# A two-layer attention and convolution kernel: position rows loaded by head, the second image issued from GpSimd, and the last 64 transform rows computed in quarters

## The chip, the core and the metric

The kernel runs on one core of one Trainium2 chip. The metric is the device time in microseconds (us) of one execution. A core has five engines with queues of their own, and in the trace an engine's instructions follow the order of its queue: TensorE (PE, matmuls; its weight loads are listed as PEld), VectorE (DVE), ScalarE (ACT), GpSimd (POOL) and SyncE (SP, which here only issues DMAs). ACT and POOL can issue DMAs too. SPq, ACTq and POOLq are an engine's sequencer, which issues DMAs and waits for semaphores.

## The reference

Two images of 128 channels and 64x64 pixels go through two layers. All data are fp32.

```python
# layer 0, on group-normalised x
y = _ln(x, g1, be1)                    # per pixel, over channels
y = _na2d(y, ...)                      # attention of each pixel to its 7x7 neighbourhood, 4 heads of 32,
                                       # with a position bias rpb[head, row offset, column offset]
y = _ln(y, g2, be2) @ w1.T + bl1; x = y + r
y = relu(_ln(x, g3, be3) @ w2.T + bl2); y = _ln(y, g4, be4) @ w3.T + bl3; x = y + r
# layer 1, on tokens t (2 x 4096 x 128)
t = t + softmax(q q^T / sqrt(128), diagonal masked) q      # q = _ln_t(t), over an image's 4096 tokens
t = t + sum over 4 branches of weight * stu(_ln_t(t)[:T/frac])   # long causal convolution with 16 filters,
                                       # by a Fourier transform, then two 128x128 matrices per filter
```

The position bias of layer 0 has 13x13 values for each head.

## The kernel before

**Layer 0** goes through 16 bands: two images, eight bands of eight image rows each. A band has 512 pixels, cut in eight tiles of 8x8; two tiles make a unit (u0 to u3). The work on a band is written as small pieces, functions with names such as `p.tok` (transpose to tokens, L327 inside `to_tokens`), `p.bn` and `p.pw` (statistics on DVE and POOL, L378 to L386), `p.za`, `p.zd` (normalise on ACT, L406, and on DVE, L415), `p.tr`, `p.zT` (transpose back, L189, and copy, L428), `p.v`, `p.q`, `p.k` (products, L466 and L332), `p.vc`, `p.qT`, `p.kT` (their copies, L474, L451, L460), and for each unit `S` (scores for four heads, L506), `t` and `e` (add the table and take the minimum on DVE, L519; exponential on ACT, L529), `T` and `c` (transpose, L542, and copy, L549) and `V` (values, L564). The order is written out by hand: PLAN gives each piece a place within a period of 2300 units for each band, and FIRST a place ahead of all for those of the first bands and for the preparations. The events are sorted by place, and PE, DVE, ACT and POOL execute them in this order. SP's DMAs follow as their data and buffers allow.

`p.vc` stores a band's v to DRAM in eight DMAs (L476), and `windows` loads for each unit the 14x14 key windows of its two tiles from there in four DMAs (L493, `vw`, six buffers). A window needs rows of the bands on both sides.

The bias is used as a table `tab` (128 queries x 196 keys) for each of six positions of a unit and each head: mask minus a shifted piece of `base`. `base` is made once per head by `flipped` (L248, the pieces `f0` to `f3`): PE multiplies `rev`, 64 shifted copies of the padded bias rows, by a flip matrix (L249), and ACT copies the result (L253). `rev` has one partition for each of the 64 query offsets, and for each head and row 20 values. It is loaded by 16 DMAs of short rows of 80 bytes (L291, L293), after two memsets. `table` (L258) makes the tables: the pieces `tab0` to `tab3` on DVE, `tab` (12 tables in 16 operations) on POOL. `weights`, `weights_kept` and `behind` fold the gains and offsets of the norms into the weights: products with one column (L721, L725) and, in `behind`, L760, L761 and L769 with small copies on DVE (L753 to L770).

The first image is loaded by four DMAs on SP at the very start (L127); group_norm takes statistics of it (L340). The second image is loaded by `second`, four DMAs on ACT's queue (L796), at place 1000.

**Layer 1** computes attention for one image after the other in pairs of 512-token chunks (L898 scores, L905 exponential, L912 transposes, L926 and L951 sums), all matmuls on PE. Between these steps `fill` puts other work: the rest of layer 0, the filters, `filter_matrices` (loads `st` on SP, mixed on DVE, L1107 to L1121), and `after`, which finishes the four tiles of 128 tokens of a chunk: divide and add (L980), normalise, transpose, and the forward transform. This transform has 320 rows, in two halves (q) of 64 input tokens: for 256 of them there are four matmuls 64x128 by 512 columns (L1011), copied on DVE for q = 0 and on ACT for q = 1 (L1013), and stored (L1000). The last 64 rows are these lines; `pu` is one PSUM bank, and `after` runs 16 times in all:

```python
pu = bank()
for q in range(2):
    rows_ = slice(q * SB, (q + 1) * SB)
    nc.tensor.matmul(pu[rows_], lhsT=tr[rows_, h, 2 * P : NC], rhs=z2[rows_], start=True, stop=True)   # L1019
ub = sp.tile([P, 512], F32, tag="ub", name="ub", bufs=3)
nc.scalar.copy(ub, pu)                                                                                  # L1021
for q in range(2):
    store(2 * P, q, ub[q * SB : (q + 1) * SB])
```

The convolution in the frequency domain follows (L1306 products with the filters, L1307 copies, L1318 the filter matrices), then the inverse transform and the output.

Of the kernel before, what the change touches and what calls it, by code (L numbers as in the profile page):

```python
# [8 lines left out]
F32 = mybir.dt.float32  # L9
# [5 lines left out]
P = 128  # L15
# [5 lines left out]
HEADS, DH, KW = 4, 32, 7  # L21
# [9 lines left out]
W_QKV, W_PROJ, W_1, W_2, W_3 = 0, 384, 512, 640, 768  # L31
V_G1, V_BE1, V_G2, V_BE2, V_G3, V_BE3, V_G4, V_BE4, V_QB, V_KB, V_BL3 = range(11)
R_VB, R_PROJ, R_BL1, R_BL2 = range(4)
RPW = 128


QT, WN, NTAB = 8, 14, 20
# [2 lines left out]
BAND = QT * GW  # L40


RPR = NTAB + 1

# [23 lines left out]


FIRST = (
    "gn p.xg0 p.xg1 p.tok0 p.tok1 w p.bn0 p.bn1 p.pw0 p.pw1 p.zd0 p.nb0 p.za0 p.tr0 p.zd1 p.nb1 p.za1 wd p.xg2 p.zT0 f0"
    " p.tr1 f1 p.v0 p.q0 p.k0 p.zT1 p.vc0 p.qT0 tab0 p.kT0 f2 f3 tab p.v1 p.k1 p.q1 tab1 p.vc1 p.kT1 p.qT1 tab2 tab3"
).split()
PHW = P + TH

# [4 lines left out]
SB = CB // SG  # L82
NC = CB + SB
# [10 lines left out]
def kernel(  # L94
# [16 lines left out]
    nc = tc.nc  # L111
# [18 lines left out]
    tt, tok, cm = [None, None], [None, None], [None, None]  # L130
# [4 lines left out]
    space = tok[0].rearrange("p n c -> p (n c)")  # L135
    base = space[:, 0 : HEADS * NTAB * NTAB].rearrange("p (h n m) -> p h n m", h=HEADS, n=NTAB)
    mask = space[:, HEADS * NTAB * NTAB : HEADS * NTAB * NTAB + 6 * KEYS].rearrange("p (c k) -> p c k", k=KEYS)
    rev = cm[0][0 : QT * QT, 0 : HEADS * RPR * NTAB].rearrange("p (h n m) -> p h n m", h=HEADS, n=RPR)

    ident = const.tile([P, P], F32, name="ident")  # L140
    make_identity(nc, ident)
# [4 lines left out]
        out=flip, in_=flip, compare_op=ALU.not_equal, fill=1.0, base=1 - QT * QT, pattern=[[0, 2], [1, QT * QT]],  # L146
# [73 lines left out]
    with l0a:  # L220
# [26 lines left out]
        def flipped(h):  # L247
            pb = l0_bank()  # L248
            nc.tensor.matmul(  # L249
                pb[:, 0 : NTAB * NTAB], lhsT=flip.rearrange("p a q -> p (a q)"),  # L250
                rhs=rev[:, h, 0:NTAB].rearrange("p n m -> p (n m)"), start=True, stop=True,
            )
            nc.scalar.copy(base[:, h].rearrange("p n m -> p (n m)"), pb[:, 0 : NTAB * NTAB])  # L253

        def table(ci, h, eng):
            n0 = (6, 0, 3)[ci // 2]
            for hp, m0 in ((slice(0, 64), 6), (slice(64, P), 0)) if ci % 2 == 0 else ((slice(0, P), 3),):
                eng.tensor_tensor(  # L258
                    tab[hp, ci, h].rearrange("p (n m) -> p n m", m=WN),
                    mask[hp, ci].rearrange("p (n m) -> p n m", m=WN),  # L260
                    base[hp, h, n0 : n0 + WN, m0 : m0 + WN], ALU.subtract,
                )
# [15 lines left out]
        )  # L278
        gavg = gavg.rearrange("p g r -> p (g r)")


        nc.gpsimd.memset(rev[:, 0].rearrange("p n m -> p (n m)"), 0.0)
        nc.gpsimd.memset(rev[:, HEADS - 1, NTAB], 0.0)
        nc.sync.dma_start(out=mask, in_=nc.inline_tensor(_window_masks(), "window_masks").ap())
        for r in range(QT):
            lo = 6 - min(r, 6)
            src = bass.AP(
                rpb_pad.tensor, (RPR + r - 6) * RPW + 50, [[1, QT], [RPW, (HEADS - 1) * RPR - r // 7], [1, NTAB]]
            )
            rows_ = rev[r * QT : (r + 1) * QT].rearrange("p h n m -> p (h n) m")  # L290
            (nc.scalar if r % 3 == 2 else nc.sync).dma_start(out=rows_[:, RPR : HEADS * RPR - r // 7], in_=src)  # L291
            src = bass.AP(rpb_pad.tensor, (lo + r - 6) * RPW + 50, [[1, QT], [RPW, RPR - lo], [1, NTAB]])
            nc.scalar.dma_start(out=rows_[:, lo:RPR], in_=src)  # L293
        wg = w_sb
        cb = wp.tile([P, 5], F32, name="cb")
        C_Q, C_K, C_V, C_1, C_3 = range(5)
# [476 lines left out]
        events = []  # L773
        for k, (b, g) in enumerate(order):
            t = {}
            for name, at in PLAN.items():
                if name[0] == "k" and b == 0:
                    continue

                at = FIRST.index(f"{name}{k}") - 1000 if f"{name}{k}" in FIRST else at + k * PERIOD  # L780
                events.append((at, k, name, lambda f=pieces[name], t=t, b=b, g=g: f(t, b, g)))
        for name, f in (
            ("gn", lambda: [None for _ in group_norm(0)]), ("w", weights), ("wd", weights_kept),
            *((f"f{h}", lambda h=h: flipped(h)) for h in range(HEADS)),
            *((f"tab{h}", lambda h=h: table(0, h, nc.vector)) for h in range(HEADS)),
            ("tab", lambda: [table(ci, h, nc.gpsimd) for ci in (1, 4, 5) for h in range(HEADS)]),
        ):
            events.append((FIRST.index(name) - 1000, None, "", f))
        for i in range(8):
            events.append((2 * PERIOD + 600 * i, None, "", lambda ci=2 + i // 4, h=i % 4: table(ci, h, nc.gpsimd)))  # L790
        rest_ = behind()
        for i in range(4):
            events.append((150 + 350 * i, None, "", lambda: next(rest_)))
        def second():
            for c in range(4):
                nc.scalar.dma_start(out=xa[1][:, c * 1024 : (c + 1) * 1024], in_=xin[1, :, c * 1024 : (c + 1) * 1024])  # L796

        events.append((1000, None, "", second))

        gn1 = group_norm(1)  # L800
        for i in range(7):
# [55 lines left out]
    with ap_:  # L857
# [6 lines left out]
        def bank():  # L864
            return ps_m.tile([P, 512], F32, tag="bank", name="bank")
# [102 lines left out]
        def after(b, c, part):  # L968

            n0 = 4 * c  # L970
            ph, f0 = divmod(n0, FB)
            par, h = divmod(ph, 2)
            pt = bank()
            for j in range(4):
                nc.tensor.transpose(pt[:, j * P : (j + 1) * P], xa[b][:, (n0 + j) * P : (n0 + j + 1) * P], ident)
            rden = sp.tile([P, 4], F32, tag="rden", name="rden")
            nc.vector.tensor_reduce(rden, part[:, n0 : n0 + 4, :], AX.X, ALU.add)
            nc.vector.reciprocal(rden, rden)
            for j in range(4):
# [15 lines left out]
            yield  # L995
            z2 = z.rearrange("p f d -> p (f d)")

            def store(m0, q, src):
                mn = min(P, NC - m0)
                nc.sync.dma_start(  # L1000
                    out=us[m0 // 2 : (m0 + mn) // 2, :, 2 * h + q, f0 : f0 + 4, b, par, :].rearrange(
                        "g r f d -> (g r) f d"
                    ),
                    in_=src.rearrange("p (f d) -> p f d", d=P),
                )

            for m0 in (0, P):
# [3 lines that stand above are left out]
                    nc.tensor.matmul(pu, lhsT=tr[rows_, h, m0 : m0 + P], rhs=z2[rows_], start=True, stop=True)  # L1011
                    ub = sp.tile([P, 512], F32, tag="ub", name="ub", bufs=3)
                    (nc.scalar.copy if q else nc.vector.tensor_copy)(ub, pu)  # L1013
                    store(m0, q, ub)
                yield
            pu = bank()
            for q in range(2):
                rows_ = slice(q * SB, (q + 1) * SB)
                nc.tensor.matmul(pu[rows_], lhsT=tr[rows_, h, 2 * P : NC], rhs=z2[rows_], start=True, stop=True)  # L1019
            ub = sp.tile([P, 512], F32, tag="ub", name="ub", bufs=3)  # L1020
            nc.scalar.copy(ub, pu)  # L1021
            for q in range(2):
                store(2 * P, q, ub[q * SB : (q + 1) * SB])
            yield

        def short_lags(b, h):
# [467 lines left out]
```

## Time and profile before

| | us |
|---|---|
| runs (3) | 2232.13, 2233.68, 2233.82 |
| median | 2233.68 |
| profiled execution | 2235.26 |
| its span | 2233.6 |
| layer 0, until the last scores and values | about 0 to 345 |
| layer 1, attention with all that is filled in | about 345 to 1330 |
| frequency domain and output | about 1330 to 2234 |

The span runs from the first to the last instruction; launch and end lie outside it. The page gives for each engine the busy time and its share, then the span in 40 slices of 55.8 us (a digit is the busy share in tenths). The chain is followed back from the last instruction: each piece is what the next one waited for. In timelines a line has start, length, engine, line, operation, `out<-in`, shapes and, in brackets, the idle time of the engine before it and what ended it. Matmuls in fp32 leave two records each. "L" with a number is a line of the kernel before.

### The profile page before, as it was taken

To read this page: it belongs to the slowest core of one execution; us is meant where nothing else is said; L and a number is where in the kernel's file an instruction comes from. 1 tells how busy PE (TensorE), PEld (TensorE's weight loads), DVE (VectorE), ACT (ScalarE), POOL (GpSimd) and SP (SyncE) were. 2 spreads that over 40 slices of the span, in tenths; PEclk is the share of its full clock that TensorE was granted. 3 is DMA by queue.
4 is the path that set the end of the run, shared out by engine and by line. 5 is a ranking of instruction groups with operands and counts; after the bars stand their busy time and mean duration, and the time that the engine had idled before them with its cause. 6 is when DMAs were issued, how large, how long until landed. Compare 5 with 4: busy or idle time off the path is not lost.

```text
span 2233.6 us, 31536 instructions
## 1 busy us (share of the span) xinstructions
PE 2165.4 (97%) x11856; PEld 1333.8 (60%) x11856; DVE 932.9 (42%) x3038; ACT 783.4 (35%) x1904; POOL 276.7 (12%) x353
## 2 busy tenths in 40 slices
PE   5899998999999999999999999999999999999998
PEld 3577774544454444544544447677677777777766
DVE  4799985434443346433333342222213232323232
ACT  2789983222332223222222332322323232222232
POOL 3367874200000000000000000000000000000000
PEclk8999998999999999999999999999999999999999
DMA  4222222011000016100000122222222121212101
GB/s 110 72 62 61 61 55 51 1 57 62 24 24 22 8 44 181 38 24 15 10 24 24 47 82 68 50 48 59 47 51 59 39 59 39 59 39 59 40 10 76
DMA packets 174810, 109.53 MB, mean 49 GB/s; under 512 B 26049, under 2 KB 159809, under 8 KB 174146
## 3 DMA queue, kind: packets, MB, share of 16 engines
q1 hardware_dynamic: 171818, 105.24, 18.0%
q10 hardware_dynamic: 2840, 2.27, 0.4%
q8 instruction: 94, 1.54, 0.3%
q14 instruction: 58, 0.48, 0.1%
HBM read 72.87 MB, written 34.60 MB: 48 GB/s over the span
## 4 chain that ended last, share of the span: by engine, by line
PE 86%; DVE 6%; POOL 3%; DMA 2%; ACT 1%; issue 1%; SPq 1%; ACTq 0%; POOLq 0%; DVEq 0%
PE acc L1318 25%; PE pc L1306 13%; PE bank L898 10%; PE own L926 10%; PE other L951 8%; PE bank L912 4%; PE bank L332 2%; PE bank L189 2%; PE bank L542 2%; PE bank L1011 1%; PE bank L1043 1%; PE py L1340 1%; DMA st<-in_m_minus_dram 1%; PE po L564 1%; PE bank L506 1%
## 5 line engine op out<-in xcount | busy, mean ns | idle before, releaser
L1307 DVE COPY y<-pc 128x512 f32<-128x512 f32 x320 | 221.6, 692 | 351.5 <-PE pc L1306 347.8
L905 ACT ACTIVATE e<-bank 128x512 f32<-128x512 f32 x288 | 171.9, 597 | 552.5 <-PE bank L898 417.3
L898 PE MATMUL bank<-cm 128*128 128x512 f32 x576 | 298.9, 603 | 1.4 <-DVE y L653 1.4
L1318 PE MATMUL acc<-y,mpl 128*128 128x256 f32 x1280 | 292.1, 382 | 0.0
L1318 PE MATMUL acc<-y,mmi 128*128 128x256 f32 x1280 | 288.0, 379 | 0.0
L1306 PE MATMUL pc<-ct,ut 64*128 64x512 f32 x1280 | 285.2, 595 | 0.9 <-issue 0.9
L1318 PEld LDWEIGHTS acc<-y,mpl 128*128 128x128 f32 x1280 | 238.1, 190 | 59.4 <-issue 29.6
L1318 PEld LDWEIGHTS acc<-y,mmi 128*128 128x128 f32 x1280 | 242.6, 190 | 32.7
L1307 ACT COPY y<-pc 128x512 f32<-128x512 f32 x320 | 205.0, 641 | 86.5 <-PE pc L1306 86.5
L951 PE MATMUL other<-e,tok 128*128 128x512 f32 x448 | 228.6, 592 | 0.0
L926 PE MATMUL own<-et,tok 128*128 128x512 f32 x448 | 227.1, 594 | 1.4 <-DVE part L915 1.4
L915 DVE CUSTOM_DVE_ANT_0 et<-bank,one 128x512 f32<-128x512 f32 x224 | 145.7, 688 | 166.5 <-PE bank L912 166.3
L1306 PEld LDWEIGHTS pc<-ct,ut 64*128 64x128 f32 x1280 | 121.5, 187 | 145.8 <-issue 140.6
L1325 ACT COPY ob<-acc 128x256 f32<-128x256 f32 x32 | 19.3, 604 | 387.0 <-PE acc L1318 387.0
L926 PEld LDWEIGHTS own<-et,tok 128*128 128x128 f32 x448 | 84.4, 190 | 109.7 <-issue 72.6
L951 PEld LDWEIGHTS other<-e,tok 128*128 128x128 f32 x448 | 85.0, 190 | 106.6 <-issue 105.9
L898 PEld LDWEIGHTS bank<-cm 128*128 128x128 f32 x576 | 95.7, 193 | 73.8 <-issue 44.7
L1342 DVE TENSOR_TENSOR xa<-py,xa 128x512 f32<-128x512 f32 x32 | 22.1, 692 | 281.4 <-PE py L1340 281.4
L912 PEld LDWEIGHTS bank<-ident,e 128*128 128x128 f32 x896 | 103.3, 142 | 57.2 <-issue 43.6
L161 POOL TENSOR_TENSOR ln_rs<-ln_rs,mhalf 128x4 f32<-128x4 f32 x24 | 24.3, 1012 | 847.6 <-DVE ln_rs L160 847.6
L529 ACT ACTIVATE p<-p,mn 128x196 f32<-128x196 f32 x256 | 114.4, 449 | 22.2 <-DVE mn L519 14.0
L912 PE MATMUL bank<-ident,e 128*128 128x128 f32 x896 | 117.6, 274 | 0.0
(208 smaller groups left out, 2292.4 us busy)
## 6 DMA issues: line engine op xcount, KB each, us to landing
ut<-us SPq DMA_DIRECT2D x80, 256.0 KB
us<-ub SPq DMA_DIRECT2D x64, 256.0 KB
vw<-vd SPq DMA_DIRECT2D x256, 49.0 KB
ct<-gs SPq DMA_DIRECT2D x160, 72.0 KB
ct<-gs SPq DMA_DIRECT2D x160, 64.0 KB
gs<-sum SPq DMA_DIRECT2D x20, 256.0 KB
vd<-v SPq DMA_DIRECT2D x128, 32.0 KB
st<-in_m_plus_dram SPq DMA_DIRECT2D x16, 256.0 KB
```

The costliest lines, as they stand in the source:

```text
L189: nc.tensor.transpose(ps[:, j * P : (j + 1) * P], src[:, j, :], ident)
L332: nc.tensor.matmul(pl, lhsT=wg[:, lo : lo + P], rhs=zT, start=True, stop=True)
L529: nc.scalar.activation(p, p, AF.Exp, bias=t[name + "mn"][:, h : h + 1], scale=-1.0, accum_out=t["den"][:, u, h : h + 1],)
L898: nc.tensor.matmul(ps, lhsT=cm[b][:, n * P : (n + 1) * P], rhs=cm[b][:, chunk(c)], start=True, stop=True)
L905: nc.scalar.activation(e, ps, AF.Exp, bias=0.0, scale=ASCALE, accum_out=part[:, n, c : c + 1])
L912: nc.tensor.transpose(pt[:, k * P : (k + 1) * P], es[k][:, m * P : (m + 1) * P], ident)
L915: nc.vector.tensor_tensor_reduce(et, pt, one, 1.0, 0.0, ALU.mult, ALU.add, part[:, n, a : a + 1])
L926: nc.tensor.matmul(own, lhsT=tok[b][:, n, :], rhs=e, start=first, stop=last)
L951: nc.tensor.matmul(other, lhsT=tok[b][:, 4 * CHUNKS[a] + j, :], rhs=es[j], start=(j == 0), stop=(j == 3))
L1306: nc.tensor.matmul(pc, lhsT=ut[fp, b, par, :], rhs=cv_[fp], start=True, stop=True)
L1307: (nc.scalar.copy if f else nc.vector.tensor_copy)(y[:, 4 * f : 4 * f + 4, :, par, b * 2 * FB + q : (b + 1) * 2 * FB : 2], pc.rearrange("p ...
L1318: nc.tensor.matmul(acc, lhsT=(mmi if l else mpl)[:, k, :], rhs=y[:, 1::2, k, ::-1, :] if l else y[:, 0::2, k, :, :], start=(l == 0 and k = ...
```

## The change

It has three parts.

1. **Position rows by head.** The padded bias has rows of 70 values in place of 128, so that one row's end is the next row's padding, and 22 rows per head in place of 21. It is copied into a DRAM tile behind six rows of its beginning. Each head's `rev` is then one DMA: 64 partitions (8 x 8 offsets), each a contiguous run of 1350 values, all issued by ACT. `flipped` reads 20 of every 70 values. The heads lie in unused space of `tt[0]` (heads 0 and 3) and `cm[0]` (1 and 2). The memsets are gone.
2. **Order at the start.** `f0` and `f1` come ahead of the first band's statistics, `f2` and `f3` around `p.tr1`, the tables earlier; `behind` runs at 900, 1200, 1500 and 1800 in place of 150, 500, 850 and 1200. The second image is issued by POOL (`x1` in FIRST, after `p.pw1`) in place of ACT at 1000.
3. **Last rows in quarters.** The last 64 rows are computed in four matmuls of 64x64 by 256 columns: q picks the input half and the bank, i the column half and the half of the output partitions. One DVE and one ACT copy of 128x256 follow, and four stores of 64 partitions in place of two.

```diff
-RPW = 128
+RPW = 70
...
-RPR = NTAB + 1
+RPR = NTAB + 2
+RLEN = (NTAB - 1) * RPW + NTAB
...
 FIRST = (
-    "gn p.xg0 p.xg1 p.tok0 p.tok1 w p.bn0 p.bn1 p.pw0 p.pw1 p.zd0 p.nb0 p.za0 p.tr0 p.zd1 p.nb1 p.za1 wd p.xg2 p.zT0 f0"
-    " p.tr1 f1 p.v0 p.q0 p.k0 p.zT1 p.vc0 p.qT0 tab0 p.kT0 f2 f3 tab p.v1 p.k1 p.q1 tab1 p.vc1 p.kT1 p.qT1 tab2 tab3"
+    "gn p.xg0 p.xg1 p.tok0 p.tok1 w f0 f1 p.bn0 p.bn1 p.pw0 p.pw1 x1 p.zd0 p.nb0 p.za0 p.tr0 p.zd1 p.nb1 p.za1 wd p.xg2"
+    " p.zT0 f2 p.tr1 f3 tab p.zT1 p.v0 p.q0 p.k0 p.vc0 p.qT0 tab0 tab1 tab2 p.kT0 tab3 p.v1 p.k1 p.q1 p.vc1 p.kT1 p.qT1"
 ).split()
...
-                rhs=rev[:, h, 0:NTAB].rearrange("p n m -> p (n m)"), start=True, stop=True,
+                rhs=rev[h].rearrange("p (n w) -> p n w", w=RPW)[:, :, 0:NTAB], start=True, stop=True,
...
-        nc.gpsimd.memset(rev[:, 0].rearrange("p n m -> p (n m)"), 0.0)
-        nc.gpsimd.memset(rev[:, HEADS - 1, NTAB], 0.0)
...
-        for r in range(QT):
-            lo = 6 - min(r, 6)
...
-            (nc.scalar if r % 3 == 2 else nc.sync).dma_start(out=rows_[:, RPR : HEADS * RPR - r // 7], in_=src)
...
-            nc.scalar.dma_start(out=rows_[:, lo:RPR], in_=src)
+        rpb = vdram.tile([(6 + HEADS * RPR) * RPW], F32, name="rpb")
+        flat = rpb_pad.rearrange("h r w -> (h r w)")
+        nc.scalar.dma_start(out=rpb[0 : 6 * RPW], in_=flat[0 : 6 * RPW])
+        nc.scalar.dma_start(out=rpb[6 * RPW :], in_=flat)
+        for h in range(HEADS):
+            src = bass.AP(rpb.tensor, rpb.offset + h * RPR * RPW + 50, [[RPW, QT], [1, QT], [1, RLEN]])
+            nc.scalar.dma_start(out=rev[h][:, 0:RLEN], in_=src)
...
+        def second():
+            for c in range(4):
+                nc.gpsimd.dma_start(out=xa[1][:, c * 1024 : (c + 1) * 1024], in_=xin[1, :, c * 1024 : (c + 1) * 1024])
...
-            events.append((150 + 350 * i, None, "", lambda: next(rest_)))
-        def second():
-            for c in range(4):
-                nc.scalar.dma_start(out=xa[1][:, c * 1024 : (c + 1) * 1024], in_=xin[1, :, c * 1024 : (c + 1) * 1024])
-
-        events.append((1000, None, "", second))
+            events.append((900 + 300 * i, None, "", lambda: next(rest_)))
...
-            pu = bank()
+            banks = [bank() for q in range(2)]
+            for i in range(2):
+                for q in range(2):
+                    rows_ = slice(q * SB, (q + 1) * SB)
+                    nc.tensor.matmul(
+                        banks[q][i * 64 : (i + 1) * 64, 0:256], lhsT=tr[rows_, h, 2 * P : NC],
+                        rhs=z2[rows_, i * 256 : (i + 1) * 256], start=True, stop=True,
+                    )
+            ub = sp.tile([P, 512], F32, tag="ub", name="ub", bufs=3)
             for q in range(2):
-                rows_ = slice(q * SB, (q + 1) * SB)
-                nc.tensor.matmul(pu[rows_], lhsT=tr[rows_, h, 2 * P : NC], rhs=z2[rows_], start=True, stop=True)
-            ub = sp.tile([P, 512], F32, tag="ub", name="ub", bufs=3)
-            nc.scalar.copy(ub, pu)
-            for q in range(2):
-                store(2 * P, q, ub[q * SB : (q + 1) * SB])
+                (nc.scalar.copy if q else nc.vector.tensor_copy)(ub[:, q * 256 : (q + 1) * 256], banks[q][:, 0:256])
+                for i in range(2):
+                    nc.sync.dma_start(
+                        out=us[P:, :, 2 * h + q, f0 + 2 * i : f0 + 2 * i + 2, b, par, :].rearrange("g r f d -> (g r) f d"),
+                        in_=ub[i * 64 : (i + 1) * 64, q * 256 : (q + 1) * 256].rearrange("p (f d) -> p f d", d=P),
+                    )
```

More of the change, by code (lines that the diff above doesn't have):

```diff
@@ L137 @@
     mask = space[:, HEADS * NTAB * NTAB : HEADS * NTAB * NTAB + 6 * KEYS].rearrange("p (c k) -> p c k", k=KEYS)
-    rev = cm[0][0 : QT * QT, 0 : HEADS * RPR * NTAB].rearrange("p (h n m) -> p h n m", h=HEADS, n=RPR)
+    place = tt[0].rearrange("p n c -> p (n c)")[0 : QT * QT, 3 * P :]
+    rev = [place[:, 0 : NTAB * RPW], *(cm[0][0 : QT * QT, h * RLEN : h * RLEN + NTAB * RPW] for h in range(2))]
+    rev.append(place[:, NTAB * RPW : 2 * NTAB * RPW])
     ident = const.tile([P, P], F32, name="ident")
@@ L279 @@
         gavg = gavg.rearrange("p g r -> p (g r)")
-        nc.gpsimd.memset(rev[:, 0].rearrange("p n m -> p (n m)"), 0.0)
-        nc.gpsimd.memset(rev[:, HEADS - 1, NTAB], 0.0)
         nc.sync.dma_start(out=mask, in_=nc.inline_tensor(_window_masks(), "window_masks").ap())
-        for r in range(QT):
-            lo = 6 - min(r, 6)
[L287 to L290, printed above, removed]
-            (nc.scalar if r % 3 == 2 else nc.sync).dma_start(out=rows_[:, RPR : HEADS * RPR - r // 7], in_=src)
-            src = bass.AP(rpb_pad.tensor, (lo + r - 6) * RPW + 50, [[1, QT], [RPW, RPR - lo], [1, NTAB]])
-            nc.scalar.dma_start(out=rows_[:, lo:RPR], in_=src)
+        rpb = vdram.tile([(6 + HEADS * RPR) * RPW], F32, name="rpb")
[5 more added lines that the diff above has]
+            nc.scalar.dma_start(out=rev[h][:, 0:RLEN], in_=src)
         wg = w_sb
@@ L785 @@
             *((f"tab{h}", lambda h=h: table(0, h, nc.vector)) for h in range(HEADS)),
-            ("tab", lambda: [table(ci, h, nc.gpsimd) for ci in (1, 4, 5) for h in range(HEADS)]),
+            ("x1", second), ("tab", lambda: [table(ci, h, nc.gpsimd) for ci in (1, 4, 5) for h in range(HEADS)]),
         ):
@@ L998, in store @@
             def store(m0, q, src):
-                mn = min(P, NC - m0)
                 nc.sync.dma_start(
-                    out=us[m0 // 2 : (m0 + mn) // 2, :, 2 * h + q, f0 : f0 + 4, b, par, :].rearrange(
+                    out=us[m0 // 2 : (m0 + P) // 2, :, 2 * h + q, f0 : f0 + 4, b, par, :].rearrange(
                         "g r f d -> (g r) f d"
```

## Prediction

> **What bounds the kernel.** I read the busy shares, the 40 slices, the table by stage, the chain that ended last, then the timeline where TensorE (PE) idles. PE first:
>
> ```profile
> PE 2165.4 (97%) x11856; PEld 1333.8 (60%) x11856; DVE 932.9 (42%) x3038; ACT 783.4 (35%) x1904; POOL 276.7 (12%) x353
> PE   5899998999999999999999999999999999999998
> ```
>
> PE is the bound nearly everywhere; its idle 68 us lie in the first slices and at the ends of the stages. So two things pay: less idle at the start, or less PE work later. The table by stage (columns: stretch, length, then busy us of PE, PEld, DVE, ACT, POOL, granted clock, DMA share, GB/s) finds a hole:
>
> ```profile
> 40.00:50.00 10.00, 9.32 (x54) 6.14 (x54) 6.42 (x33) 3.03 (x11) 5.05 (x7) 0.53 0.36 111
> 50.00:60.00 10.00, 3.51 (x11) 2.03 (x10) 0.14 (x2) 4.90 (x19) 0.00 (x0) 0.50 0.62 203
> ```
>
> From 50 us all compute stops for about 5 us; the PE clock is 0.5. The chain (start, us, what) and ACT's timeline name the cause:
>
> ```profile
> 47.47 0.72 SPq L493
> 48.24 5.98 DMA vw<-vd
> 54.22 0.02 issue
> 54.24 0.34 ACTq L796
> ...
> 56.59 1.95 PE bank L542 x8
> 58.53 1.71 PE bank L332 x2
> 60.24 0.97 PE po L564 x32
> ```
>
> ```profile
> 47.66 7.40 ACTq L796 DMA_DIRECT2D xa<-in_x_dram  x3
> 55.10 0.46 ACT L529 ACTIVATE p<-p,mn 128x196 f32<-128x196 f32 x1 [7.49 <-DMA vw<-vd]
> ```
>
> ACT issues the second image (L796). Its third DMA waits for a window load (vw) issued by SP at 48.24 and landing at 54.22, slow because the image's first half moves at that time. Behind it in ACT's queue stand the exponentials L529, for which PE's transposes L542 wait.
>
> **What the Trainium skill says.** "DMA: Bandwidth & Descriptors", section "Issuing engines are not separate DMA queues": DMAs of SP, ACT and GpSimd run on the same engines and interleave; another issuer saves only sequencer time. The trace agrees: SP's vw load is held by ACT's image. So the gain of moving the image is in who waits, and in when it moves. "TensorEngine Tiling (Array Packing)", "Tiling Modes": 64x64 gives four tiles that work in parallel; "Gotcha 1": different row tiles write different PSUM banks. The trace has both, below. "TensorE: Matmul & The Clock Gate", Part 1: PE runs at half clock until a window of some 3.4 us was busy. Here the clock is half from 40.57 to 61.05, six such windows.
>
> **Part 1, second image.** Today four ACT DMAs (0.36 us each) plus the wait. Changed: GpSimd issues them after the second `p.pw`, which ends at 19.9 us, and no wait stands before them. The transfer, 2 MB at the 290 GB/s seen at 48 to 50 us, is some 7 us, about 21 to 28 us, where the DMA share is 0.00; v's stores come after. Behind it in POOL's queue stand 16 table operations of 0.6 us (9.6 us), the last twelve of which need the fourth flipped head. The trace shows no GpSimd DMA; the skill's DMA page (Bandwidth; "Latency and other measured facts") gives 1 us of emission to the first byte. Bounds of POOL's hold: 0 (the other work waits for ACT anyway) to the 7 us of the transfer. Even at 7 the tables start at 27 and end at about 37, before the second unit needs them (42 below). I take zero on the path.
> Gain: PE idles 6.49 us before L542 at 56.59. With ACT free it follows the transposes that end at 50.1: **6.5 us**.
>
> **Part 2, rows by head and new order.** It removes the two POOL memsets (0.55 us, hidden), and the 16 row DMAs (six on SP, ten on ACT) become six on ACT: two copies, 26 KB in all, into a DRAM buffer, then four of 64 rows by 5400 B = 346 KB. SP's six stood where it waits for v anyway (17.7 to 29.5 us). As built, the load of w_sb now waits for the first copy, about 6 us; it landed at 10.7, is due at 16.57 and may come at 12. Bytes rise from 0.41 to 1.38 MB, but in rows of 5400 B, not 80 B. The loads of xa land at 4.2, 5.7, 8.2 and 9.5 us, and the last stands before the statistics at 9.55; row DMAs that overlap it delay everything by as much. The first ACT packets moved 3.7 us after their issue while xa was queued, so the copies land at about 6 us and the rows flow when xa is nearly through: 0.3 us, bounds 0 and 1.5. All early bytes (2.1 + 0.46 + 0.6 + 1.38 MB) at the 350 GB/s of 4 to 8 us end near 15 us.
> The flips f0, f1 move ahead of the first normalised transposes:
>
> ```profile
> 21.31 1.25 PE L189 MATMUL bank<-ident,z 128*128 128x128 f32 x4 [2.95 <-ACT z L406]
> 22.49 1.70 PE L249 MATMUL bank<-cm,flip 64*128 64x400 f32 x2
> ...
> 31.30 1.61 PE L249 MATMUL bank<-cm,flip 64*128 64x400 f32 x4
> ```
>
> A flip cost 1.65 us at 22.5 us and 0.8 at 31.3, with one form: PE was at half clock before the first clock record at 30.3, though the table's clock column shows 1.00 there. Two now fill PE's idle from 18.36 to 21.31, end at 21.7, their ACT copies (0.49) at 22.25, so z (ACT L406), before at 20.80, starts 1.45 us late, and v0 and SP's stores with it: 29.5 becomes 30.9. The table load (1.28 us before L406) leaves the path, as ACT's first use is now a copy without that wait; it is in these times. In return no flip stands between k0 and v1 (1.6 us), and all four DVE tables but one come before kT0. kT1 then ends at 35.0 in place of 35.8, and 2.34 us of tables behind it are gone: the first score (L519) starts at 36.8 instead of 39.28, the first band's four exponentials end at 39.3, not 41.8.
> Before, PE then ran the weight products L760 and L761 (41.17 to 43.34) ahead of the transposes; they are moved behind the next scores, where PE waits for DVE. Transposes 43.34 become 39.3: 4.0 us. Half-clock products there (2.2 us) and the later one (0.4) come back partly: I leave **3.0 us** net at the second unit's transposes (bounds 1.8, if all 2.2 return, and 4.0), less 0.3 for xa, less 0.6 for the last product and a clock window that may close later: **2.1 us**.
> Part 1 and 2 together, at the first V product (60.2 us): **8.6 us** earlier. What is late next? SP. It issues a store per 0.61 us and a load per 0.77 us: 16 stores and 22 loads from 30.9 end at 57.6, against 62.8 before. The third v's stores, at 64.69 before, could start at 56.1 by PE, at 57.6 by SP. The second band's first V needs them, two loads (1.5) and about 2.5 us to land: 66.6, and PE asks at 68.3. It holds by 1.7 us. Per band SP needs 8 x 0.61 + 16 x 0.77 = 17.2 us, PE's period is 18.05, so the shift lasts.
>
> **Part 3, last rows in quarters.** Two 64x64 matmuls of 512 columns become four of 256, sixteen times:
>
> ```profile
> 482.95 1.08 PE L1019 MATMUL bank<-z,tr 64*64 64x512 f32 x4
> 483.96 1.09 PE L912 MATMUL bank<-ident,e 128*128 128x128 f32 x8
> ```
>
> ```profile
> 63.97 0.59 PE L506 MATMUL bank<-kT,qT 32*64 32x196 f32 x16
> 64.49 0.65 PE L564 MATMUL po<-pT,vw 98*32 98x64 f32 x32
> ```
>
> Each fp32 matmul leaves two records. The first takes PE 1.00 us. The second is eight 32x64 matmuls on four row and two column groups in 0.52 us; in the records all eight start within 45 ns, the second passes 0.22 us later: column halves run together. The 512-column passes are 0.43 us long, so four quarters in two passes of 0.21 with the same 0.15 around them take 0.57: 0.43 x 16 = 6.9 us of PE work. ACT's copy 128x512 (0.59) becomes one of 256 there and one on DVE (0.415, as L764), 6.6 us on DVE beside PE. Two more stores each (0.5 us of SP, which idles there). One bank more is held. Bounds: 0 (no overlap, or PE waits for banks) and 6.9; near DVE's waits for `st` loads at 838 to 912 us some is lost. I take **5.8**.
>
> **Sum.** 8.6 + 5.8 = 14.4. The profiled execution took 2235.26 (span 2233.6), 1.6 above the median of the runs, 2233.68. The sum is made in its times and gives 2220.9 for it; on the median it gives 2219.3.
>
> **Rivals.**
> (a) The quarters gain nothing: the copy on DVE is queued behind mixing that waits for DMA, and PE waits for its bank. For it: DVE's waits of 3 us at 838 to 912. Against: only two of sixteen calls lie there. 8.6 alone: 2225.
> (b) Another wait takes the place of ACT's: SP (1.7 us of room) or POOL's descriptors. The start keeps 4, with the quarters 9.8: 2224.
> (c) Slower: the rows, read from overlapping addresses 4 bytes apart, move like today's 80-byte packets (36 to 46 GB/s at 12 to 20 us). At 36 GB/s 1.38 MB take 38 us; from xa's last landing at 9.5 the fourth head is in at 47.5. Its flip is due on PE at 26.6 and v0 stands behind it: 20.9 us late, 2219.3 + 20.9 = 2240. It decides from 14.4 us late. Against it: the rows are 5400 B, and larger packets moved at 350.
> (d) SP's stream, which is on the chain from 29.5 to 48.2 us, is the true bound; it starts 1.4 us later, the first V product moves with it, and the quarters are hidden: the stall's place changes and its sum does not, 2233.7 plus at most 1.4.
>
> **Chances.** Forecast 0.64 (own range 2215 to 2223), (a) 0.16, (b) 0.13, (c) 0.03, (d) 0.04. The measurement tells about 0.2%, 4.5 us, from no change: faster 0.93, same 0.04, slower 0.03. The range 2214.5 to 2227 takes in both bounds of part 3 and the start's, 5 to 10.5 us.
>
> **What would show it.** After: no xa entry in ACT's queue and no 7.4 us hole, first V product near 51.5 us, scores from 36.8; the quarters, eight records, over in 0.57 us; POOL's tables over by 37. Wrong if f0 waits for rows on PE, if xa's last load lands past 11 us, if a POOL entry lasts beyond 7 us, or if PE waits for `bank` at the quarters.

## The result and the profile after

The changed kernel takes 2224.51 us in the median (2223.36 to 2226.62), the kernel before 2234.49 beside it: a ratio of 0.9952 (95% interval 0.9942 to 0.9963). Measured again, it was 0.9955 (0.9941 to 0.9968). That is 10 to 11 us faster; 14.4 were forecast, and the own range of the forecast, 2215 to 2223, is missed by 1.5. The profiled execution took 2225.03, its span is 2223.3.

First the page of the changed kernel, busy shares and TensorE's slices, then its table by stage (columns as before). Its L numbers differ by up to eleven from those of the kernel before: L1020 holds the quarters, L565 the values, L494 the window loads, L785 the second image.

```profile
PE 2160.3 (97%) x11920; PEld 1335.6 (60%) x11920; DVE 938.2 (42%) x3054; ACT 778.6 (35%) x1904; POOL 278.1 (13%) x355
...
PE   6899998999999999999999999999999999999998
```

```profile
40.00:50.00 10.00, 9.50 (x60) 6.46 (x58) 4.11 (x25) 5.79 (x21) 0.00 (x0) 0.50 0.21 60
50.00:60.00 10.00, 9.01 (x166) 6.75 (x156) 5.84 (x31) 7.05 (x22) 3.32 (x5) 0.99 0.23 66
```

Between 50 and 60 us PE is busy for 9.01 us in place of 3.51, at full clock: the hole has gone. GpSimd's timeline shows where the image went, and the last tables behind it:

```profile
19.58 2.41 POOL L785 DMA_DIRECT2D xa<-in_x_dram  x4
...
28.14 7.86 POOL L262 TENSOR_TENSOR tab<-tok 128x196 f32<-128x196 f32 x13 [1.92 <-ACT tok L257]
```

Four issues cost GpSimd 2.41 us, the image has landed at 28.5, and the tables are done at 36.0. Eight records of one call of quarters take PE 0.59 us (the next line starts at 838.71), where the old pair took 1.00 to 1.01:

```profile
838.12 0.66 PE L1020 MATMUL bank<-z,tr 64*64 64x256 f32 x8
838.71 1.13 PE L898 MATMUL bank<-cm 128*128 128x512 f32 x2
```

So the image and the quarters did locally what was forecast. The first score starts at 35.6 us, in the repeated run at 37.2 (36.8 forecast), and no flip waits for its rows. The chain of the changed kernel names what is late next (start, us, what):

```profile
64.24 0.73 SPq L494
65.02 0.73 SPq L494
65.80 2.50 DMA vw<-vd
68.34 0.32 PE po L565 x8
```

PE has 24 of 32 value records of the second band's first unit done at 67.0 and waits until 68.34 for the last window half. In this trace SyncE's queue, gapless from 30.2 us, is the next limit. In the trace of the repeated run it is not: there PE is 3 us later at this place, and all 32 records run without a wait:

```profile
69.54 0.65 PE L565 MATMUL po<-pT,vw 98*32 98x64 f32 x32
```

To see where 14.4 became 10, I subtract the start of the same PE instruction in the kernel before (us; negative is earlier). The second trace is of the repeated run.

| reached | before, at | forecast | first trace | second trace |
|---|---|---|---|---|
| first V product | 60.2 | -8.6 | -10.6 | -7.5 |
| third band's first V | 95.9 | -8.6 | -8.1 | -7.4 |
| layer 1, ahead of the first quarters | 399.7 | -8.6 | -6.7 | -7.2 |
| ahead of the filter loads | 804.0 | | -8.7 | -9.3 |
| behind them | 917.3 | | -9.4 | -10.3 |
| ahead of the last chunks | 1283.1 | | -11.7 | -12.7 |
| frequency domain begins | 1330.2 | -14.4 | -10.8 | -11.9 |
| end of the span | 2233.6 | -14.4 | -10.2 | -11.4 |

A call is one pass of the quarters in `after`. The shift should grow by 0.42 at each of the 16 calls, 6.7 in all; over the 14 calls up to 1283 us it grows by 5.0 and 5.5 of 5.9. Shift is lost at the second band's windows (first trace), at about 204 us (0.7 in the first trace, where PE waits 0.46 us for a window load), at the layer border (335 to 370; 1.0 in the first trace) and, by 1.6 to 1.7, at 1286; at the filter loads (804 to 917) it grows by 0.7 and 1.0 where three calls should bring 1.3. My theory after this reading: the work saved is near the forecast, and waits and TensorE's half-clock stretches (granted clock 0.5) take part back. The rivals: the quarters lose it by their extra copy and stores, or the start by SyncE.

### The profile page after: what moved, and what is told of

Read it like the earlier page. It is cut to its first block, busy times and chain, and to the rows that moved or that the text cites. A ratio compares the mean times of both kernels' runs of the same rounds, so it can differ in the third digit from the quotient of the medians.

```text
span 2223.3 us, 31764 instructions
## 1 busy us (share of the span) xinstructions
PE 2160.3 (97%) x11920; PEld 1335.6 (60%) x11920; DVE 938.2 (42%) x3054; ACT 778.6 (35%) x1904; POOL 278.1 (13%) x355
## 4 chain that ended last, share of the span: by engine, by line
PE 86%; DVE 6%; POOL 4%; DMA 2%; ACT 1%; issue 1%; SPq 1%; POOLq 0%; DVEq 0%; ACTq 0%
PE acc L1326 25%; PE pc L1314 13%; PE bank L898 10%; PE own L926 10%; PE other L951 8%; PE bank L912 4%; PE bank L333 2%; PE bank L193 2%; PE bank L1010 2%; PE bank L1051 1%; PE bank L543 1%; PE py L1348 1%; PE bank L507 1%; ACT p L530 1%; DVE ln_st L379 1%
## 5 line engine op out<-in xcount | busy, mean ns | idle before, releaser
L926 PE MATMUL own<-et,tok 128*128 128x512 f32 x448 | 227.3, 594 | 1.7 <-DVE part L915 1.7
L926 PEld LDWEIGHTS own<-et,tok 128*128 128x128 f32 x448 | 84.3, 190 | 110.5 <-issue 72.3
L898 PEld LDWEIGHTS bank<-cm 128*128 128x128 f32 x576 | 95.9, 193 | 73.4 <-issue 43.7
```

The lines of the kernel that those rows point to most:

```text
L898: nc.tensor.matmul(ps, lhsT=cm[b][:, n * P : (n + 1) * P], rhs=cm[b][:, chunk(c)], start=True, stop=True)
L926: nc.tensor.matmul(own, lhsT=tok[b][:, n, :], rhs=e, start=first, stop=last)
```

## The experiments

All times are medians; ratios are against the kernel before on the same chip.

**Quarters alone.** On the kernel before, the third part of the change and nothing else:

```diff
-            pu = bank()
-            ...
+            banks = [bank() for q in range(2)]
+            ...
```

> The kernel before with the last rows in quarters, and nothing else. My theory: the quarters are worth what TensorE needs less per call, 1.01 - 0.59 = 0.42 us, sixteen times 6.7 us, and only half-clock stretches of TensorE (3.4 us each, up to 1.7 us of loss), which fall differently in each execution, make it more or less: about 2227.5 against 2234.3, between 2226 and 2230. Rival 1: the extra copy on DVE or the second bank gives part back between 870 and 1290 us (the trace of the changed kernel loses 2.3 us there): a loss that comes with every run, 4.4 us of gain, about 2230. Rival 2, from the prediction: no gain, 2234.

Measured: 2234.42 against 2235.54, ratio 0.9991 (0.9985 to 0.9998): 0.4 to 3.4 us, not 6.7. The trace has the 0.59 us calls. Up to 804 us the five calls bring 2.0. Then between 804 and 917, where three calls should bring 1.3, it loses 2.4, and 1.7 at 1297. I count as the cost of half-clock stretches half of the time that PE is busy in them. That is the most they can take: where PE would have waited anyway, it takes less. They cost 4.4 us in that part in place of 1.7; a slice shows one (clock 0.66):

```profile
835.00:840.00 5.00, 5.00 (x12) 2.03 (x12) 2.70 (x8) 1.68 (x2) 0.00 (x0) 0.66 0.69 182
```

By this count 1.0 us of the 3.7 remains, and there is something that I had not priced. The order in this part of layer 1 is not written by hand: a scheduler sets it when the program is built, and the quarters move more than themselves. DVE's order in the two traces, with the value copies (`et`, for which the sums L926 wait) against the filter mixing:

```
before                                  quarters alone
mpl<-st,wt                              et,part<-bank,one  (two)
et,part<-bank,one  (two)                mmi<-mdiff,sg, mpl<-mpl,sg ... (five)
mpl<-st,wt,mpl x3                       mpl<-st,wt
mmi<-st,wt                              mpl<-st,wt,mpl x2
xa<-bank,seg,xa; xa<-other              xa<-bank,seg,xa; xa<-other
mmi<-st,wt,mmi x2                       mpl<-st,wt,mpl
xa<-bank,seg,xa                         mmi<-st,wt
et,part<-bank,one  (two)                xa<-bank,seg,xa
                                        et,part<-bank,one  (two)
```

From the start of its first to the start of its last instruction that reads a load, the mixing takes 74.1 us before, 80.4 here, 77.4 in the changed kernel (77.0 in its second trace). The order and the half-clock stretches were not varied one without the other, so this split is read from the trace and not shown by a run.

**Start alone.** On the changed kernel, the reverse:

```diff
-            banks = [bank() for q in range(2)]
-            ...
+            pu = bank()
+            ...
```

> The changed kernel with the last rows as before: position rows by head, new order and second image on GpSimd. My theory: the start's 10.6 us at the first V product become 8 once the second band waits for its windows, and about 6.7 at the border of the layers, so 2227 to 2228 against 2234.3; no half-clock stretch at 1286 us unless its grid happens to fall so. Rival: the start keeps all 10.6 and it is the quarters that lose 4: 2224.

Measured: 2229.99, 0.9972 (0.9962 to 0.9983), 6.3 us. Its shift is 8.3 at the first V product and at the third band, 8.1 at 399.7, and 7.7 at the end. Beside the changed kernel's two measurements (10 to 11 us) the quarters add about 4 here, between their 2 alone and the 6.7 of their products.

**Image alone.** The kernel before with one piece moved:

```diff
-p.bn0 p.bn1 p.pw0 p.pw1 p.zd0
+p.bn0 p.bn1 p.pw0 p.pw1 x1 p.zd0
...
-                nc.scalar.dma_start(out=xa[1]...
+                nc.gpsimd.dma_start(out=xa[1]...
```

> The kernel before with only the issue of the second image moved from ScalarE at place 1000 to GpSimd after the second p.pw. My theory: the hole of 7.4 us in ScalarE's queue goes, the transposes of the second unit start at 50.1 in place of 56.6, the first V product at 53.8 in place of 60.2 (6.5 earlier); SyncE's stores still start at 29.5, so its loads end near 57 and the second band loses about 1 of it: 4.5 to 6 in the time, 2229. Rival: the stall moves on to the window loads on SyncE and nothing is left of it, 2234. Second rival: GpSimd's descriptors for 2 MB hold its tables, and the scores with them: later than 39.3 us.

Measured: 2228.24, 0.9966 (0.9953 to 0.9978), 7.6 us (4.9 to 10.5). The second unit's transposes start at 49.8, the first V product is 7.8 earlier, the third band's 7.4. So one moved piece brings what all of the start brings (6.3 above; the intervals overlap). The traces show where the lead of the new order ends. In the first trace of the changed kernel the first V product comes 2.8 us earlier than here, and PE then waits 1.33 us for SyncE's windows. The new order doesn't make SyncE's stream earlier; here it reads:

```profile
29.44 10.21 SPq L476 DMA_DIRECT2D vd<-v  x16
39.70 17.18 SPq L493 DMA_DIRECT2D vw<-vd  x22
56.98 4.96 SPq L476 DMA_DIRECT2D vd<-v  x8
```

Here the third band's stores start at 56.98, in the changed kernel at 57.46: the stream starts with v0 (29.44 against 30.19) and runs without a gap. In the changed kernel's second trace and in that of the start alone, half clock lasts longer at the start, to 53.3 and 51.9 us in place of 50.3. The first V product comes at 52.6 and 51.9, about as late as here (52.3), and in these three traces PE waits for no window at the second band. Either way the third band's first V comes at 87.6 to 88.5 us.

Image alone and quarters alone sum to 9.6 us, about what the changed kernel gains. A kernel with these two and without rows and order was not run, so it isn't shown that rows and order bring anything to the whole.

**Image back on ScalarE.** On the changed kernel, `x1` out of FIRST, and:

```diff
-                nc.gpsimd.dma_start(out=xa[1]...
+                nc.scalar.dma_start(out=xa[1]...
...
+        events.append((1000, None, "", second))
```

> The changed kernel with the second image issued by ScalarE at place 1000 again, as before. My theory: the hole in ScalarE's queue comes back, because a window load is in flight there as well; 5 to 7 us at the first V product, of which the second band's wait for SyncE hides 1.5 or less: 2228 to 2230 against 2224.5. Rival: with the rows off SyncE's and ScalarE's queues the image finds its semaphore free and the hole is 2 us or less: 2225 to 2226.

Measured: 2229.36, 0.9969 (0.9957 to 0.9982). It lies in the expected range, 3 to 5 us slower than the changed kernel; the hole is back, in ScalarE's queue and in the chain:

```profile
45.63 6.74 ACTq L785 DMA_DIRECT2D xa<-in_x_dram  x3
52.41 0.46 ACT L530 ACTIVATE p<-p,mn 128x196 f32<-128x196 f32 x1 [10.35 <-DMA xa<-in_x_dram]
```

```profile
46.45 5.56 DMA vw<-vd
52.03 0.34 ACTq L785
```

The first V product is only 3.0 earlier than before. The rival (a hole of 2 us or less) falls. With the image on ScalarE rows and order do bring something (6.9 us here against 2.0 for the quarters alone); with it on GpSimd no gain of theirs is seen (6.3 against 7.6). The parts do not add.

**The changed kernel again.**

> The changed kernel once more, for the spread of one kernel from one execution to the next and for a second trace. My theory: TensorE's half-clock stretches lie on a grid of 3.413 us that falls differently in each execution, so the stretch at 1286 us (1.65 us lost) need not come again, and the times spread over some 3 us about 2224.5. Rival: it belongs to the changed kernel, comes in every trace at the same work, and the spread has another cause.

Measured: 2223.92 (2223.40 to 2226.51), 0.9955. The stretch at 1286 came again, and one at 828 that the first trace lacks. In ten traces of nine kernels the wait ahead of the last chunk but one of both images is 1.60 us long (TensorE idle until DVE's z). In every trace the clock changes only on a grid of 3.413 us, whose phase differs from trace to trace. The Trainium skill, "TensorE: Matmul & The Clock Gate", Part 1, says so: a free-running window of 3413 ns. It has the clock fall after an idle window of that length; here a wait of 1.60 us inside one window was enough, so on this the measurement decides. Where in its grid window the wait began separates the cases:

| wait began, us into its window | half-clock stretch follows |
|---|---|
| 0.04, 0.20, 0.41, 0.60, 0.62, 0.65, 0.89, 0.93, 0.99 | yes, 9 of 9 |
| 1.11, 1.19, 1.24, 1.62, 1.90, 2.08, 2.57, 2.88, 2.91, 2.97 | no, 0 of 10 |
| 3.32 | yes |

The boundaries were read from these 20 waits. The one such wait of a further kernel (the first try of filled waits, below) began at 1.32 and has no stretch. If the grid falls evenly, the table makes it about one such wait in three (1.1 of 3.4 us, an estimate; here it was 10 of 20), at up to 1.7 us each. The trace of the kernel before has none at these two places, those of the changed kernel one and two: the loss at 1286 is the draw of the traces and not the change. The times spread over 3.1 us, as expected; that the stretch came at 1286 twice is where the grid fell (0.65 and 0.04), and two other kernels with the quarters and the same wait there have none (1.24 and 2.08).

**Quarter stores on GpSimd.** On the changed kernel, for the four stores of a call:

```diff
-                    nc.sync.dma_start(
+                    nc.gpsimd.dma_start(
                         out=us[P:, ...
```

> The changed kernel with the four quarter stores of each call issued by GpSimd in place of SyncE. My theory: on SyncE the two more stores per call stand ahead of the filter loads, and DVE waits for these loads (3.4 us of its waits in 820 to 925 us stand at the first mix of a row of filters, none in the kernel before); with SyncE free of them that wait goes, TensorE's wait for the normalised rows falls from 5.4 to about 4 us, and the time by 1 to 2 us against the changed kernel: 2223. Rival: the loss is made by the second copy on DVE and by half-clock stretches, SyncE has room: no change, 2224.5.

Measured: 2225.53, 0.9962 (0.9949 to 0.9974): no gain. The mixing takes 75.0 us in place of 77.4, so the stores did lengthen it, and TensorE's wait for the normalised rows falls from 5.4 to 4.5 us, but the time doesn't fall. What the expectation says of the kernel before is wrong: its wait at the first mix is 2.5 us and not none (changed kernel 3.4, here 2.9). No gain is what the rival said; its cause was not tested.

**Filled waits, first try.** On the changed kernel, ahead of the transposes of the normalised rows:

```diff
+            if c == 7 - b:
+                pt = bank()
+                for _ in range(3 if b else 8):
+                    nc.tensor.matmul(pt, lhsT=ident, rhs=cm[b][:, 0:512], start=True, stop=True)
             pt = bank()
             transposed(pt, z)
```

> The changed kernel with products that nobody reads on TensorE where it waits for the normalised rows of the last chunk but one of the second image (1283 us, three of 128x512) and of the last chunk of the first image (845 us, eight). They add work and take none away. My theory: the half-clock stretches that follow these two waits (848.9 to 852.4 and 1285.9 to 1289.3) come from TensorE's idleness; with the waits filled they are gone and the time falls by up to 1.6 each: 2221 to 2223. Rival: the clock falls for another reason, and the added work costs 0 to 0.5: 2224.5 to 2225.

Measured: 2230.06, 0.9980 (0.9973 to 0.9987), 6 us slower than the changed kernel. I had mis-sized the fill: an fp32 product of 512 columns leaves two records and takes 0.85 us, so the eight took 6.8 us, and they read memory that the filter mixing takes over:

```profile
845.18 7.03 PE L991 MATMUL bank<-cm,ident 128*128 128x512 f32 x16
```

```profile
852.25 0.49 DVE L1119 TENSOR_SCALAR mpl<-st,wt 128x512 f32<-128x512 f32 x1 [5.54 <-PE bank L991]
```

In its trace neither filled wait is followed by a half-clock stretch, but the waits are no longer those of the changed kernel, so this run settles nothing on the clock.

**Third band's stores, half of them on GpSimd.**

```diff
-                nc.sync.dma_start(
+                (nc.gpsimd if (b, g) == (0, 2) and i % 2 else nc.sync).dma_start(
```

> The changed kernel with four of the eight stores of the third band's v issued by GpSimd, idle from 40 to 56 us, in place of SyncE. My theory: SyncE is what is late after the start; its stream gets 2.4 us shorter there, the second band's windows land before TensorE asks, and the 1.3 us wait at 66.5 to 68.3 goes; with the idle of 2 us that follows at 75 to 78 also the half-clock stretch at 77.6 may go: 1 to 2.5 us less, 2222 to 2223.5. Rival: the next wait (DVE's and GpSimd's share of the same band) takes it back, no change.

Measured: 2230.24, 0.9977 (0.9970 to 0.9984), 6 us slower. The stores wait for ScalarE's copy of v, and the next band's `xg` stands behind them in GpSimd's queue; PE waits for it (3.12 and 1.17 us, until 60.9 and 62.6):

```profile
57.61 2.40 POOL L477 DMA_DIRECT2D vd<-v  x4 [18.77 <-ACT v L475]
60.06 2.45 POOL L437 TENSOR_SCALAR xg<-xa,gm,grs 128x128 f32<-128x128 f32 x2
```

In the changed kernel this `xg` ran at 37.3. I had called GpSimd idle and not asked what its next instruction was.

**The same relief, with `xg` ahead of the stores.** One line more:

```diff
+                at = 160 if (name, k) == ("p.xg", 3) else at
```

> The changed kernel with four stores of the third band's v on GpSimd as in the run before, but with the third x of the next band (xg3), which stood behind them in GpSimd's queue and came 20 us late, placed ahead of them, where GpSimd is idle from 40 us. My theory: SyncE's stream is 2.4 us shorter at 60 us, the second band's first values no longer wait for their windows (1.3 to 1.6 us), and 1 to 2.5 us are gained: 2222 to 2223.5. Rival: DVE, busy all of 72 to 76 us, becomes the wait, and the time stays at 2224.

Measured: 2224.19 (2221.01 to 2225.23), 0.9947 (0.9934 to 0.9960). The wait is gone, all 32 records run as one:

```profile
66.73 0.65 PE L565 MATMUL po<-pT,vw 98*32 98x64 f32 x32
67.32 1.12 PE L333 MATMUL bank<-zT,w_sb 128*128 128x512 f32 x2
```

The third band is 10.2 us earlier than before, against 8.1 and 7.4. But the relief counts only where PE comes early. The trace here is like the first one of the changed kernel (first V product at 49.46 and 49.57), and against that SyncE was the next limit. In the second one PE reaches these records at 69.54 and has no wait to lose. Of the 2.1 us more than in the first trace 0.9 is left at 399.7 (7.6 against 6.7); at the end the shift is 11.2 (10.2 and 11.4 in the two traces of the changed kernel). In the time of the whole kernel it is not told apart from the changed kernel.

**Filled waits, sized rightly.** On the changed kernel; likewise three of 512 columns ahead of the last `k.b` (wait until 357), in an edit that is not printed here:

```diff
             pt = bank()
+            n, w = {6: (2, 384), 7: (0 if b else 4, 512)}.get(c, (0, 0))
+            for _ in range(n):
+                nc.tensor.matmul(pt[:, 0:w], lhsT=ident, rhs=tt[b][:, n0 : n0 + w // P, :]..., start=True, stop=True)
             transposed(pt, z)
```

> The changed kernel with unread products in four of TensorE's waits, written into the bank that the waiting transposes overwrite: three of 128x512 (0.85 us each) ahead of the last tokens of the first image (wait of 2.63 us to 357.4), two of 384 columns ahead of the normalised rows of each image's last chunk but one (waits of 1.60 us to 827.8 and 1284.7), four of 512 ahead of those of the first image's last chunk (3.83 us to 849.2). They add work and take none away. My theory: the half-clock stretches at 357, 828 or 849 and 1286 us (2.8, 1.6 and 1.7 us of loss in the two traces of the changed kernel) come from idle stretches of TensorE; filled, they are gone, and the time falls by 3 to 6 us: 2218.5 to 2221.5. Rival: the clock falls for another reason; the time stays at 2224 or is up to 1 us later.

Measured: 2230.55, 0.9978 (0.9967 to 0.9988): 6 us slower, where 3 to 6 faster were expected. The clock part came true in this trace: the stretches at 357, 828, 849 and 1286 are all gone, and half-clock with PE busy, from 62 us to 2200 us, costs 3.4 us in place of 10.6. A slice of the changed kernel, then one of the filled kernel (clock is the third last column):

```profile
849.00:852.40 3.40, 3.15 (x8) 1.51 (x10) 1.98 (x9) 1.28 (x2) 0.00 (x0) 0.50 0.66 191
```

```profile
847.00:853.00 6.00, 5.47 (x23) 2.78 (x23) 4.15 (x15) 2.20 (x4) 0.14 (x1) 1.00 0.83 225
```

At 804 us it is 11.6 earlier than the kernel before (changed kernel 8.7 and 9.3). But at 917 it is 4.7. PE's waits from 780 to 925 us, changed kernel, then filled:

```profile
PE bank L193 <- DVE z L182: 6.2, 3, 3.8
PE own L926 <- DVE part L915: 1.4, 4, 0.6
```

```profile
PE own L931 <- DVE part L920: 7.3, 6, 1.9
PE bank L996 <- DVE tt L985: 1.7, 1, 1.7
PE bank L193 <- DVE z L182: 1.5, 3, 0.7
```

With the fill the scheduler built another order on DVE between the loads, and now value copies stand behind a mix that waits for its load. For one of these waits, DVE's timeline:

```profile
882.13 0.75 DVE L1128 SCALAR_TENSOR_TENSOR mmi<-st,wt,mmi 128x512 f32<-128x512 f32 x1 [1.04 <-DMA st<-in_m_minus_dram]
...
885.81 0.68 DVE L920 CUSTOM_DVE_ANT_0 et<-bank,one 128x512 f32<-128x512 f32 x1
```

So my theory is half right: idleness of PE makes these stretches; but the kernel is not 3 us faster without them, as the fill, like the quarters, comes with another order on DVE, and a worse one. Fill and order were not varied one without the other.

**Both together.** The relief and these fills, both edits as above.

> The two edits before this one together, on the changed kernel. My theory: they act at different places and add: 4 to 8 us, 2216.5 to 2220.5. Rival: with TensorE ahead at 68 us the idle stretches fall elsewhere and half-clock stretches with them: no better than the filled kernel alone.

Measured: 2231.17, 0.9979 (0.9970 to 0.9987). They do not add. From 804 to 917 it loses 6.3, like the filled kernel. The relief moved nothing here: PE came late (first V product at 51.93), and the third band is 7.7 us earlier than before, the filled kernel's without relief 7.5. No better than the filled kernel is what the rival said; its reason is not what the trace shows.

**Quarters alone, filled.** The kernel with the quarters alone, with the same fills.

> The kernel before with the quarters alone (2.0 us of gain where 6.7 were in the products) and the same four fills. My theory: about half of what the quarters lose is half-clock stretches at 365, 836 to 863 and 1297 us (6 to 7 us of loss in that trace, 4.8 in the kernel before); filled, the time falls to 2229 to 2231. Rival: the quarters are lost to DVE, which waits for the filter loads between 840 and 920 us: the fills change less than 1 us, 2234.

Measured: 2237.71, 1.0007 (0.9999 to 1.0015): 3 us slower than unfilled, and the half-clock cost is 3.0 us in place of 11.9; at the places that the expectation names, the unfilled trace has 8.9 and not 6 to 7. One stretch of 3.4 us, at 365.6, stayed behind a filled wait. PE waits 7.5 us for `part` in 845 to 925: what the fill gives on the clock is lost there, as before. Neither theory foresaw a slower kernel; the rival's cause, DVE at the filter loads, is the nearer one.

## Why the prediction was right, and where it missed

Direction and range held: 2224.5 lies between 2214.5 and 2227, 5 us above the forecast of 2219.3 and above its own range (2215 to 2223). The gain is the image's and part of the quarters'.

- **Part 1, 6.5 us.** Right: 7.6 (4.9 to 10.5) alone, by the mechanism named: ScalarE's queue is free, GpSimd issues in 2.41 us, no descriptor wait. Put back on ScalarE, the image brings the hole back.
- **Part 2, 2.1 us.** Wrong as a term of a sum. At the first V product the changed kernel is at -10.6 and -7.5 (-8.6 forecast; the two traces differ in when TensorE's clock first rises, 29.8 and 32.9 us). The forecast lies between them, and neither trace has it. Beyond that, image alone and whole start give the same within their intervals. In the traces, what the new order gains ends in SyncE's wait where TensorE comes early, and in a longer half-clock stretch at the start where it doesn't.
- **"It holds by 1.7 us."** The sum behind it is wrong. I counted two loads for the second band's first V. The chain shows four issues of 0.8 us before the last one's 2.5: landing at 68.3 and not 66.6. Where PE asked at about 67.0 it waited 1.3 us, which is rival (b)'s SyncE wait, and taking that away moved the third band by 2 us. Where PE asked later than the forecast's 68.3, as in the second trace, nothing waited, and that is luck.
- **Part 3, 5.8 us.** The products were sized well (0.57 forecast, 0.59 measured; 6.7 in all), and no PE wait for a bank at the quarters appeared. What is lost around them was sized too small: I had taken 1.1 off. By the medians they give 2.0 alone and about 4 on the start. Alone, 3.7 are lost between 804 and 917 us, where two things lie that the sum left out: the scheduler's other order around the filter mixing, and half-clock stretches. Their shares are not settled. On the start, in the two traces, only 0.6 and 0.3 are lost there, and the one large loss is the stretch at 1286.
- **The clock.** Half-clock stretches between 62 and 2200 us cost 10.6 and 10.7 us in the two traces of the changed kernel, 7.9 in that of before: at most 2.7 of the missing 4. The count is a weak measure of time: it gives 13.2 in the trace of image alone and 6.6 in that of the start alone, whose spans differ by 1.2 us. Part of it (1.7 to 3.4) depends on where the grid falls, which a sum from one profile can't know.
- **The rivals.** 2224.5 is nearer to what (b) and (a) named, 2224 and 2225, than to the forecast. This is chance: (a) gave the quarters nothing and they bring 2 to 4, (b) left the start 4 and it brings 6.3, though the SyncE wait that (b) names is there in one of the two traces. (c) and (d) did not come: no flip waited for its rows, and SyncE's wait took 1.3 us at 67 us and 0.5 at about 204, not the whole gain.

What stays open: why the layer border (335 to 370) takes 1.0 of the shift in one trace and 0.2 in the other, how much of the quarters' loss is order and how much is clock, and whether rows and order are worth anything beside the image.

## What to carry to other kernels

Two gains at the start need not add: follow the next late stream from its own first instruction, count its issues per consumer, and take the smaller shift. Before a wait is called the next limit, see whether a second trace of the same kernel has it. Where a scheduler sets part of the order, an added instruction moves others; compare the built orders of every engine before you price it at "hidden". Before a stream is put on an idle engine, ask what that engine's next instruction is and who waits for it.

## What the runs showed of the hardware that was not expected

- A wait of 1.60 us on TensorE was followed by a half-clock stretch when it began in the first 1.0 us of a 3.413 us grid window (9 of 9), and not when it began 1.1 to 3.0 us into it (0 of 10); one that began at 3.32 was. A stretch of 3.4 us with PE busy costs up to 1.7, an estimate: a flip product took 1.65 us at half clock and 0.8 later.
- With unread products in four such waits (2.6, 1.3, 3.4 and 1.3 us), two traces of the filled kernels have no stretch at these places, where the two of the changed kernel have 6.0 and 7.7 us of half-clock cost; a third kept one.
- GpSimd issued four DMAs of 512 KB in 2.41 us, 0.60 each; ScalarE took 0.36 for one.
